# A two-layer graph network with residual and layernorm: the order of each engine's instructions from a planner at build time, and layer 1's products in float32r halves, two node tiles to a pass

## The chip, the cores and the metric

The kernel runs on one core of one Trainium2 chip. The core has a matrix engine (TensorE, PE in the profile, with PEld for its weight loads), a vector engine (VectorE, DVE), a scalar engine (ScalarE, ACT), a general one (GpSimd, POOL) and SyncE (SP), which here only issues transfers. Each executes its own list of instructions in the order in which the program issued them; semaphores connect the lists. The metric is the device time of one execution in microseconds, the median of several.

## The reference

There are 6250 nodes with 256 features, and 100000 edges sorted by destination. Destinations are drawn as 6250 u², u uniform, so low-numbered nodes have many more edges than high-numbered ones. In float32:

```
def agg(h, eps):                 # GIN aggregation
    return (1 + eps) * h + segment_sum(h[src], dst)
h   = relu(agg(x, eps1) @ W1a + b1a)     # 256 -> 512
h1  = relu(h @ W1b + b1b)                # 512 -> 512
h   = relu(agg(h1, eps2) @ W2a + b2a)    # 512 -> 512
y   = h @ W2b + b2b                      # 512 -> 256
out = layernorm(x + y)                   # eps 1e-5, no scale or shift
```

## The kernel before, in words

Nodes come in 49 tiles of 128 (the last has 106). Edges come in chunks of 128. Both layers have the same structure, and each aggregation is done in two ways.

*Edges to higher nodes* (502 chunks) are gathered: POOL issues one indirect DMA per chunk (`gather`, L262 to L278, the DMA at L270), which fetches 128 rows of x or of h1. Chunks come in pieces of four, six pieces are in flight, and piece i + 6 may not be issued before the sums of piece i. PE adds the 128 rows into at most 32 slots by a product with a 0/1 matrix `sel` (L1087). Groups of up to 20 chunks make one such set of sums; ACT copies it (`split`, L1111, or L535 and L536 in layer 2), PE spreads it over 128 nodes by a second 0/1 matrix `to` (L1136), and DVE adds it to the accumulators `acc` of the tiles it reaches (L1125). Groups run from the highest nodes to the lowest.

*Edges to the seven lowest tiles* ("heavy", 280 chunks) are counted. DVE makes two 0/1 masks per chunk, `ca` (L919) and `cb` (L922), PE multiplies them (L961), and DVE adds the counts to `at` at an offset read at run time (L935). The table `at` holds four node tiles in a ring (`RING`); ACT turns a tile's counts into float32 (`cf`, L946), stores them as uint16 for layer 2 (L951), and DVE zeroes the place for the tile four further down (L948). PE then multiplies the counts of a tile by all 49 tiles of x, in 13 ranges of four node tiles (L869). Layer 1 does this in float32, one heavy tile after the other, and reads x anew for each. Layer 2 loads the stored counts and takes h1 as two float32r halves: `upper`, rounded by ACT (L535), and the rest, by DVE (L536).

*Dense work* is done on blocks of one or two tiles (`block`, L717): transposes (L746), a copy `zt` (L755), the first product (L778), relu with bias (`ht`, L787), the second product (L799), and the finish: layer 1 adds the bias on DVE (L1162), applies relu on ACT (L1166) and writes h1; layer 2 adds bias and residual and normalises (L1191 to L1208). Accumulators are loaded by `seed` (L616) into eight block buffers and scaled by ACT (L634).

Layer 2's gathers read arbitrary rows of h1, so the first of them waits for the last write of layer 1.

The order of each engine's list is set while the kernel is built, with the framework's own scheduling off. One loop goes through the pieces (L1071 to L1150). Four times per piece it calls `tick`, which issues what `later` and `take_later` have put off by a fixed number of chunks (`LAG`, ten or seven), and `pump`, which lets two queues, the dense blocks and the heavy tiles' work, issue a step each time their credit allows. `spread` (L124) sets the credit rates, so that dense and heavy work together take an even share.

## Time and profile before

| | us |
|---|---|
| median of three runs | 1387.91 (1386.85 to 1388.59) |
| the profiled execution's time | 1388.87 |
| its span, first to last instruction | 1387.0 |
| layer 1's first and last gather issued | 8.78 and 672.88 |
| layer 2's first and last gather issued | 705.38 and 1348.36 |

In the profile's rows, the number after the start is a duration; brackets hold the idle time before the instruction and what ended it. A row of stretches gives the busy time of each engine with its count of instructions, then the granted PE clock (1.00 is full), the busy share of the DMA engines and GB/s. A row of waits gives the total, the count and the longest. Records of consecutive matmuls overlap, so their mean is more than the time each adds; runs of them in the chain of waits give that time. A float32 matmul has two records.

### The profile page before, as it was taken

The page shows a single profiled execution, that of the slowest core. Times are in us where ns is not written, and L with a number is a line of the kernel's source. Part 1 is how long each engine was busy: PE and PEld are TensorE (multiplying, and loading weights), DVE is VectorE, ACT ScalarE, POOL GpSimd, SP SyncE. Part 2 cuts the span into 40 slices and gives each one's busy share as a digit, 9 for nine tenths or more (in the row PEclk, how much of TensorE's full clock was granted, in tenths as well). Part 3 has the DMA queues.
Part 4 walks back from the last instruction along what each step waited for, and adds up shares of the span by engine and source line. Part 5 has one row for each costly group of instructions (what it writes and reads, how often), then busy time and mean ns, then how long its engine had stood idle before and what let it go on. Part 6 is the DMA issues. An engine that isn't in the chain of part 4 may idle for free.

```text
span 1387.0 us, 19481 instructions
## 1 busy us (share of the span) xinstructions
PE 1264.6 (91%) x6366; PEld 799.7 (58%) x6366; DVE 851.8 (61%) x2208; ACT 457.5 (33%) x871; POOL 975.1 (70%) x1018
## 2 busy tenths in 40 slices
PE   2579999999998999999853999999999999999897
PEld 1136566465655656555531576676666666666666
DVE  7985675768666686711122768868876565665334
ACT  0234253343523324242232333433443333322121
POOL 6777776677677677777347777777777776777760
PEclk9989999999999999999986999999999999999999
DMA  4668687586775847785379797998898898977771
GB/s 110 194 213 267 199 252 245 159 251 202 243 236 168 275 154 223 213 277 179 119 274 302 248 307 248 303 300 286 251 321 291 281 306 275 305 238 233 233 236 41
DMA packets 181091, 328.05 MB, mean 237 GB/s; under 512 B 26425, under 2 KB 112631, under 8 KB 180981
## 3 DMA queue, kind: packets, MB, share of 16 engines
q0 software_dynamic: 64256, 197.46, 45.9%
q1 hardware_dynamic: 94312, 103.36, 22.9%
q10 hardware_dynamic: 22412, 25.89, 5.4%
q8 instruction: 54, 0.88, 0.3%
q14 instruction: 57, 0.46, 0.1%
HBM read 296.18 MB, written 30.44 MB: 235 GB/s over the span
## 4 chain that ended last, share of the span: by engine, by line
PE 79%; DVE 9%; DMA 6%; POOL 2%; issue 2%; ACT 1%; DVEq 0%; ACTq 0%; SPq 0%; POOLq 0%
PE bank L869 21%; PE bank L799 18%; PE bank L778 17%; PE bank L1087 12%; PE bank L1136 5%; PE bank L961 3%; PE bank L746 2%; DMA early<-h,srcs 2%; DMA late<-h,srcs 2%; DVE at L935 2%; POOL early L270 1%; DMA xr<-in_x_dram 1%; DVE acc L1125 1%; DVE cb L922 1%; POOL late L270 1%
## 5 line engine op out<-in xcount | busy, mean ns | idle before, releaser
L270 POOL DMA_INDIRECT early<-in_x_dram,srcs x502 | 487.8, 972 | 182.8 <-issue 124.7
L270 POOL DMA_INDIRECT early<-h,srcs x250 | 240.8, 963 | 112.4 <-issue 95.1
L869 PE MATMUL bank<-xr,cf 128*128 128x256 f32 (+2 forms) x1029 | 304.7, 392 | 13.6 <-DMA xr<-in_x_dram 4.3
L270 POOL DMA_INDIRECT late<-h,srcs x252 | 243.9, 968 | 78.3 <-issue 63.1
L1125 DVE SCALAR_TENSOR_TENSOR acc<-bank,mask,acc 128x256 f32<-128x256 f32 (+1 forms) x420 | 231.4, 607 | 80.6 <-PE bank L1136 80.4
L869 PEld LDWEIGHTS bank<-xr,cf 128*128 128x128 f32 (+1 forms) x1029 | 196.0, 193 | 57.8 <-issue 12.4
L778 PE MATMUL bank<-zt,w2a_s 128*128 128x256 f32 (+2 forms) x832 | 178.8, 373 | 2.1 <-ACT zt L755 2.1
L799 PE MATMUL bank<-w1b_s,ht 128*128 128x512 f32 (+1 forms) x392 | 176.7, 598 | 0.0
L778 PEld LDWEIGHTS bank<-zt,w2a_s 128*128 128x128 f32 x832 | 151.9, 194 | 36.0 <-DVE acc L1125 3.9
L1087 PE MATMUL bank<-early,sel 128*32 128x256 f32 (+1 forms) x1504 | 152.2, 479 | 19.2 <-DVE sel L654 10.1
L869 PE MATMUL bank<-upper,cf 128*128 128x512 f32 (+1 forms) x343 | 143.2, 417 | 14.6 <-DMA ci<-counts 11.6
L1136 PE MATMUL bank<-split,to 128*128 128x256 f32 (+3 forms) x360 | 120.3, 438 | 24.7 <-ACT split L535 21.1
L935 DVE TENSOR_TENSOR at<-bank,at 128x490 f32 x173 | 115.3, 667 | 32.8 <-PE bank L961 14.0
L799 PEld LDWEIGHTS bank<-w1b_s,ht 128*128 128x128 f32 (+1 forms) x392 | 73.4, 191 | 86.3 <-issue 79.7
L1136 PEld LDWEIGHTS bank<-split,to 128*128 128x128 f32 (+1 forms) x360 | 65.7, 199 | 73.6 <-ACT split L535 28.6
L876 DVE TENSOR_TENSOR acc<-bank,acc 128x512 f32<-128x512 f32 (+1 forms) x98 | 64.8, 665 | 65.8 <-PE bank L869 65.5
L922 DVE TENSOR_SCALAR cb<-numbers,spot 128x490 f16<-128x490 f16 x280 | 103.1, 368 | 0.0
L654 DVE TENSOR_TENSOR sel<-iota,slot 128x256 f32<-128x256 f32 (+2 forms) x118 | 50.7, 430 | 84.1 <-PE bank L1087 83.3
L536 DVE TENSOR_TENSOR split<-bank,split 128x512 fp32r<-128x512 f32 (+1 forms) x90 | 61.1, 681 | 64.0 <-ACT split L535 63.9
L869 PEld LDWEIGHTS bank<-upper,cf 128*128 128x128 f32 (+1 forms) x343 | 65.1, 190 | 58.7 <-ACT cf L886 17.5
L961 PE MATMUL bank<-cb,ca 128*128 128x490 f16 x280 | 87.7, 381 | 10.0 <-DVE at L935 6.5
L778 PE MATMUL bank<-zt,w1a_s 128*128 128x256 f32 (+2 forms) x416 | 94.2, 373 | 1.4 <-DVE at L935 1.0
(128 smaller groups left out, 1286.5 us busy)
## 6 DMA issues: line engine op xcount, KB each, us to landing
xr<-in_x_dram SPq DMA_DIRECT2D x84, 512.0 KB
h<-h1r ACTq DMA_DIRECT2D x48, 256.0 KB
xr<-h SPq DMA_DIRECT2D x12, 1024.0 KB
acc<-h SPq DMA_DIRECT2D x22, 512.0 KB
counts<-ci ACTq DMA_DIRECT2D x84, 128.0 KB
ci<-counts SPq DMA_DIRECT2D x84, 128.0 KB
early<-in_x_dram,srcs POOLq DMA_INDIRECT x502
acc<-in_x_dram SPq DMA_DIRECT2D x22, 256.0 KB
```

The source lines that it names most:

```text
L270: nc.gpsimd.indirect_dma_start(out=rows_[:, j, :], out_offset=None, in_=table, in_offset=bass.IndirectOffsetOnAxis(ap=srcs[:, c : c + 1], ...
L536: nc.vector.tensor_tensor(lower, of, upper, op=ALU.subtract)
L778: nc.tensor.matmul(ph[0][:, (f - o) * TILES * P : (f - o) * TILES * P + nb], wa[:, k, f * P : (f + 1) * P], zt[:, k, :nb], start=(k == 0), ...
L799: nc.tensor.matmul(po[0][:m], ht[:, f, i * P : i * P + m], wb[:, f, :], start=(f == 0), stop=(f == KH - 1),)
L869: nc.tensor.matmul(pm[0], cf[:m, j, :], of[:m, j, :], start=(opens and j == 0 and of is not (None if once else xr)), stop=(closes and j == ...
L876: nc.vector.tensor_tensor(acc[t], ap, acc[t], op=ALU.add)
L922: made = nc.vector.tensor_scalar(b, numbers, spot[:, c : c + 1], None, op0=ALU.is_equal)
L935: nc.vector.tensor_tensor(to, ap.rearrange("p (k w) -> p k w", w=W), to, op=ALU.add)
L961: mm = nc.tensor.matmul(pc[0], a, b, start=(i == 0), stop=(i == n - 1))
L1087: mm = nc.tensor.matmul(pm[b * SLOTS : (b + 1) * SLOTS], sel[:, c - c0, :], rows_[:, j, :], start=(c == parts[b][0]), stop=(c == parts[b][ ...
L1125: nc.vector.scalar_tensor_tensor(acc[t], ap[:, i * width : (i + 1) * width], mask[:, t - lo[g], g : g + 1], acc[t], op0=ALU.mult, op1=ALU.add,
L1136: nc.tensor.matmul(pu[0][:, i * width : (i + 1) * width], to[:used], split[:used, l, :], start=(once or l == 0), stop=(once or l == 1),)
```

## The change

**The order.** `Queue`, `later`, `tick`, `pump`, `place` and `spread`'s rates no longer set it. Each piece of work becomes a Python generator that asks for an engine (with an estimated cost and a priority), for a buffer, for an event, or for a rest (an estimated transfer time). A small event simulation, `Plan`, runs while the kernel is built, and grants each engine to the waiting request of the lowest priority number; an instruction is issued at the moment of the grant. On PE the order of priority is: sums of gathered rows (0); merges, counting and layer 1's products (1); dense blocks (2); layer 2's products (3). On DVE and ACT merges come first, and masks and counts last. Nothing of the simulation remains at run time: each engine executes a fixed list and waits on semaphores as before.

```
+LINK = {"PE": 0.4, "DVE": 0.2, "ACT": 0.3}
+GATHER = 1.255
+LANDINGS = (3.0, 6.0)
+LOAD = 6.0
+SUMS = 0.0025
+MERGE = 0.25
+ENDING = 3
+def dve(n):
+    return 0.15 + 0.00105 * n
+def act(n):
+    return 0.18 + 0.00083 * n
...
+    def grant(self, e):
+        if self.free[e] <= self.now and self.asks[e]:
+            _, _, process, cost = heapq.heappop(self.asks[e])
+            self.free[e] = self.ending = self.now + cost
+            ask = self.advance(process)
+            if ask:
+                self.at(self.ending + LINK[e], self.take, process, ask)
+            self.at(self.free[e], self.grant, e)
...
+                    yield ("until", arrived[upto])
+                    yield ("on", "PE", SUMS * width, 0)
...
+                        yield ("on", "ACT", act(n * P) + 0.1, 3)
```

**Layer 1's products.** They use float32r. In the first of four passes (tiles 6 and 5; 4 and 3; 2 and 1; 0) each range of x is loaded, ACT rounds it to one half, DVE forms the other, and both are stored to a new DRAM tile `halves`; the later passes load both halves and ACT copies them once more as float32r. One matmul covers both halves, 512 columns wide, and DVE adds both halves of the result.

```
-                        for of in (xr,) if once else (upper, xr):
-                            nc.tensor.matmul(
-                                pm[0], cf[:m, j, :], of[:m, j, :],
...
+                                yield ("on", "PE", PASS * len(ks) * 2 * width, 1)
...
+                                    nc.tensor.matmul(
+                                        bank[tokens[i].number][:, : 2 * width], cf[:m, j, :],
+                                        xh[:m, j, :, :].rearrange("p a d -> p (a d)"),
+                                        start=(k == 0), stop=(k == NT - 1),
+                                    )
...
+                    for i in range(2):
+                        yield ("on", "DVE", dve(width), 2)
+                        nc.vector.tensor_tensor(
+                            acc[t], ap[:, i * width : (i + 1) * width], acc[t], op=ALU.add
+                        )
```

Four checks of the node numbers are added to the preparation, because counting for a later pass may begin before the ring's old places are cleared, as far as the edges allow.

**Layer 1's finish.** The bias comes in as a float32r matmul of 64 rows, which opens the second product; ACT's relu then reads PSUM directly, and the DVE addition is gone.

```
+                            nc.tensor.matmul(po[:m], twice[:, :m], bias, start=True, stop=False)
...
-            nc.vector.tensor_tensor(y[:m], po[:m], b1b_s[:m], op=ALU.add)
```

**Counting.** The `ca` masks are made for four chunks by one tensor_tensor. Cleared places of `at` are zeroed by ACT, not DVE:

```
+                    yield ("on", "ACT", act(here.shape[1] * P), 4)
+                    nc.scalar.activation(here, here, AF.Copy, scale=0.0)
```

**Layer 2.** Its products go through the ranges from the highest nodes down. The heavy tiles' accumulators start as ACT copies of the first product, and the tile's own scaled rows are added by DVE later (`sowing`, 60 us on). Its plan starts 40 us before its gathers. Tiles that the last three groups reach become blocks of one tile in both layers. Buffers that layer 1 needs only for the heavy tiles, and those that layer 2 needs early, lie in the same part of the memory (`loan`).

More of the change, by code (lines that the diff above doesn't have):

```diff
@@ L27 @@
 RANGE = 4
+PAIR = 2
+BATCH = 4
 PACES = (1.15, 1.4)
@@ new lines, in layer, with settle @@
+            block_of = {t: b for b, ts in enumerate(blocks) for t in ts}
+            passes = PASSES if once else ()
+            need = [
+                sum(uses[t] + ((1 if once else len(ranges)) if t < tiles else 0) for t in ts) + 1
+                for ts in blocks
+            ]
+            acc = {}
+            ready = {t: Event(plan) for t in range(NT)}
+            def settle(t):
+                b = block_of[t]
+                need[b] -= 1
+                if not need[b]:
+                    plan.then(plan.start, dense(b))
@@ L608, in layer @@
[L608 to L636 removed]
+            arrived = {}
```

1386 lines of the change are left out of this document (863 added, 523 removed).

## The prediction

> **What bounds the kernel now.** I read the shares of busy time first, then four stretches cut at the first and last row gather of each layer, then the rows of GpSimd (POOL), which issues the gathers, and its waits, last the chain at the two ends.
>
> ```profile
> PE 1264.6 (91%) x6366; PEld 799.7 (58%) x6366; DVE 851.8 (61%) x2208; ACT 457.5 (33%) x871; POOL 975.1 (70%) x1018
> ```
>
> ```profile
> 8.70:674.00 665.30, 609.00 (x2967) 360.62 (x2968) 428.30 (x1265) 226.88 (x414) 487.79 (x502) 0.98 0.69 214
> 674.00:705.30 31.30, 23.04 (x108) 13.55 (x106) 5.03 (x10) 11.04 (x24) 0.00 (x0) 0.89 0.30 105
> 705.30:1349.50 644.20, 603.61 (x3110) 401.94 (x3111) 399.53 (x791) 211.38 (x411) 484.72 (x502) 0.96 0.86 279
> 1349.50:1387.00 37.50, 28.02 (x181) 23.04 (x180) 14.73 (x38) 8.15 (x23) 0.00 (x0) 0.92 0.16 49
> ```
>
> ```profile
> 8.78 1.13 POOL L270 DMA_INDIRECT early<-in_x_dram,srcs  x1 [5.50 <-DVE rawf L343]
> ...
> 672.88 0.95 POOL L270 DMA_INDIRECT early<-in_x_dram,srcs  x1 [0.30 <-issue]
> 705.38 0.94 POOL L270 DMA_INDIRECT early<-h,srcs  x1 [31.55 <-issue]
> 706.62 0.95 POOL L270 DMA_INDIRECT early<-h,srcs  x1 [0.30 <-issue]
> ...
> 1348.36 0.95 POOL L270 DMA_INDIRECT late<-h,srcs  x1 [0.30 <-issue]
> ```
>
> PE is 91% busy and looks like the bound. POOL is at 70%, yet each gather carries 0.30 us of issue that isn't counted: 0.95 + 0.30 = 1.25 us is the undisturbed step. Layer 1's 501 steps take 672.88 - 8.78 = 664.1 us, 1.326 each; layer 2's take 1348.36 - 705.38 = 643.0 us, 1.283 each. So 501 steps at 1.25, 626 us, are a wall in each layer, and the kernel is two such walls, a hand-over of 31.55 us between them and an end of 37.5 us. What is above the wall is partly PE: a gather reuses its buffer only when PE has summed the rows there.
>
> ```profile
> POOL early L270 <- PE bank L1087: 23.1, 20, 5.7
> POOL early L270 <- PE bank L961: 12.4, 16, 6.0
> ```
>
> ```profile
> POOL early L270 <- PE bank L1087: 6.7, 6, 3.8
> ...
> POOL late L270 <- PE bank L1087: 3.0, 5, 1.7
> ```
>
> The first fence is layer 1, the second layer 2. Take the ordinary 0.30 from each count: 35.5 - 36 x 0.30 = 24.7 us lost to PE in layer 1, 9.7 - 11 x 0.30 = 6.4 in layer 2. The rest above the wall (664.1 - 626 - 24.7 = 13 and 643.0 - 626 - 6.4 = 11) is longer gathers, and stays. The change can therefore win about 31 us inside the layers, plus what it wins at the ends.
>
> **The change, part by part.**
>
> ```profile
> L869 PE MATMUL bank<-xr,cf 128*128 128x256 f32 x672 | 164.9, 390 | 13.6 <-DMA xr<-in_x_dram 4.3 <-ACT ht L787 3.7 <-ACT split L1111 2.8
> ```
>
> ```profile
> 389.44 1.92 PE bank L869 x8
> ...
> 1085.35 1.85 PE bank L869 x8
> ```
>
> *Layer 1's products.* A float32 matmul is two records, so 672 records are 336 full products, four to a range and tile: 1.92 us. Layer 2 already has float32r products 512 wide: eight took 1.85 us, 0.23 each. (The mean of 390 ns is no price; pipelined records overlap.) The new form needs 4 x 0.23 = 0.93 us where 1.92 stood, so 343 products save 343 x (0.48 - 0.23) = 85 us. The bias as a matmul adds 49 x 0.23 = 11 us, so PE gives up 74 us in layer 1: 609 - 74 = 535 us of work for 640 us of gathering. Even if the plan wastes a tenth of PE, the gathers bound this layer. Of the 24.7 us I take 20 (bounds 0 and 24.7; a loss is the second rival).
>
> ```profile
> L1162 DVE TENSOR_TENSOR h1t<-bank,b1b_s 128x512 f32<-128x512 f32 (+1 forms) x49 | 33.7, 688 | 97.3 <-PE bank L799 97.1
> L919 DVE TENSOR_SCALAR ca<-numbers,low 128x128 f16<-128x128 f16 x280 | 76.3, 273 | 12.7 <-PE bank L961 12.7
> L922 DVE TENSOR_SCALAR cb<-numbers,spot 128x490 f16<-128x490 f16 x280 | 103.1, 368 | 0.0
> L948 DVE MEMSET at<- 128x256 uint32 (+1 forms) x39 | 10.1, 260 | 16.6 <-ACT cf L946 15.1
> L946 ACT CAST cf<-at 128x512 f32<-128x512 uint16 (+1 forms) x91 | 54.1, 595 | 113.2 <-DVE at L935 80.6 <-PE bank L869 13.6 <-DMA xr<-in_x_dram 4.3
> ```
>
> ```profile
> 746.16 1.15 ACT L634 ACTIVATE acc<-acc,e 128x1024 f32<-128x1024 f32 x1 [27.77 <-DMA acc<-h]
> ```
>
> *DVE and ACT.* DVE loses the bias addition (33.7), the memsets (10.1) and 280 small `ca` masks (76.3) for 70 of four times the width, each between 0.37 (the 490-wide mask) and 0.69 (a 512-wide tensor_tensor): 26 to 48 us; I take 48. It gains 13 subtractions for the halves of x, 1024 wide, two of 0.69 each: 18 us; and 7 second additions. In all about -50 on 428. ACT gains 13 halving casts (1.15 each at 1024 wide, 15 us), 39 rounding copies of reloaded halves at twice that (90 us) and 39 clearings at 0.6 (23 us): 227 becomes about 355 of 640. Neither fills up, so both cost nothing while PE and the gathers run beside them. If that cover were gone, ACT's 2.3 us rounding copies would stand ahead of a merge's copy in ACT's queue, and the gathers' 24 rows of buffer would have to pay.
>
> ```profile
> xr<-in_x_dram SPq DMA_DIRECT2D x84, 512.0 KB
> ```
>
> *DMA.* Seven readings of x (84 x 0.5 MB = 42 MB in whole ranges) become one reading, one storing of halves and three readings at 1 MB a range: 12 x (0.5 + 1 + 3) = 54 MB. 12 MB more on 214 GB/s x 665 us = 142 MB: the DMA share goes from 0.69 to about 0.75, below the 0.86 at which layer 2's gathers keep 1.283. Nothing on the path. The new loads pass SP's queue beside the accumulator loads; a load waiting there for a free buffer holds up the next seed, as 84 such loads do now.
>
> *The start.* Four more checks are eight small DVE instructions before the branch, some 2 us. The first 24 gathers run on beside it, but the first sums then come later by up to that. I take +1 (0 to 2).
>
> ```profile
> 677.44 1.00 PE bank L1087 x16
> 678.44 3.65 PE bank L799 x8
> 682.08 0.02 issue
> 682.11 0.70 DVE h1t L1162
> 682.81 0.02 issue
> 682.83 0.64 ACT h1r L1166
> ...
> 683.86 0.59 ACT split L1111
> 684.45 0.04 issue
> 684.50 2.07 PE bank L1136 x4
> ...
> 700.90 0.70 DVE h1t L1162
> ```
>
> *The hand-over.* The last sums end at 678.44, and their copy by ACT starts at 683.86: in ACT's written order it stands behind the relu of an older tile, which waits for DVE, which waits for PE. The plan gives a merge's copy first place. That takes out up to 5.4 us, and the two bias additions on this chain 1.4 more; the bias matmuls put back 0.5. Take -5 (-9, with a tighter end, to +4, where an older tile's last block comes to stand before the final ones). Layer 2's PE work no longer stands still after it:
>
> ```profile
> 750.88 1.51 PE L1136 MATMUL bank<-split,to 64*128 64x512 f32 x2 [21.11 <-ACT split L535]
> ```
>
> ACT waits 27.77 us there for accumulator rows that SP fetched late, and PE 21.11 us behind ACT. The new kernel issues them ahead, and starts its products with the high ranges, written long before. That frees PE, but POOL lost only 6.4 us in this layer: take -4 (-6.4 to 0). The heavy tiles' own rows are now added by seven DVE instructions some 60 us later instead of scaled by ACT at the start; DVE is busy 399.5 of 644.2 us there, so they hide.
>
> ```profile
> 1356.97 0.99 PE bank L1087 x8
> 1357.96 3.77 PE bank L778 x32
> 1361.73 0.69 PE bank L1136 x2
> ```
>
> ```profile
> 1357.89 3.84 PE L778 MATMUL bank<-zt,w2a_s 128*128 128x128 f32 x32
> ...
> 1366.66 5.47 PE L778 MATMUL bank<-zt,w2a_s 128*128 128x128 f32 x32 [2.08 <-ACT zt L755]
> ```
>
> *The end.* The last gather leaves at 1349.3; its sums run at 1356.97 behind other tiles' blocks, and the merge behind another 3.77 us. Sums and merges come first in the plan, some 6 us sooner, but the heavy tiles' blocks must still find room: -5 (-9 to +6).
>
> Sum: -20 + 1 - 5 - 4 - 5 = -33 us on a span of 1387.0, to 1354. This execution took 1388.87, 1.9 more than its span; the median of the runs is 1387.91. From the median: 1355.
>
> **The rivals.**
>
> *PE stays the bound in layer 1.* The last fence shows the same 32 records take 3.84 us, and 5.47 after an idle 2.08: a gap costs 1.6 us more, at a lower clock. The freed 105 us (640 - 535) may come as gaps of some 2 us; 105 / 3.7 = 28 of them eat it. Then layer 1 keeps its 664 us, and only the ends win: -13, 1375. For it: the plan is exact where the chip is not. Against it: a gap at which PE waits for rows means that POOL is the bound already, and the gathers run 24 rows ahead. The Trainium skill (TensorE: Matmul & The Clock Gate, "What's actually happening") says that the clock halves only after an idle window of about 3.4 us; by that rule such gaps cost nothing more and the sum stands. The row above disagrees, with 2.08 us.
>
> *Slower: the heavy tiles' chain outlasts the gathers.* Counting must finish two tiles before their pass, and tiles share a ring of four, so counting for 2, 1 and then 0 waits until 6, 5 and then 4 are copied out and cleared. A pass takes ACT 13 x (2 x 3 x 0.6 + 2.3) = 77 us; two such waits are 153. DVE has about 378 us of work in this layer and counting stands last in its order, so with no idle time at all it ends near 31 + 378 + 153 = 562, and the last pass near 562 + 13 x 3.5 = 608, 45 before the gathers' new end near 653. DVE now idles 665 - 428 = 237 us. Let 90 of these fall into the chain, and it ends 45 us late; with its block of 12 us the hand-over slips by some 50: 1405. It is slower than before once it slips by 33. Against: counting need not wait for all of a pass, and DVE's other work isn't all ahead of it.
>
> *No change worth measuring.* The plan's costs miss, its first-come order hands back at merges and seeds what it wins: 1388.
>
> **How the numbers follow.** The forecast 0.68 (own range 1338 to 1373: all bounds that gain, -24.7 - 9 - 6.4 - 9 = -49, give 1339); PE still the bound 0.12; no change 0.07; the slow chain 0.13. Below 0.2%, 2.8 us, a measurement of this kernel tells nothing. Of the no-change case 0.06 lies within that and 0.01 beyond it on the fast side. Faster: 0.68 + 0.12 + 0.01 = 0.81; same 0.06; slower 0.13. A range of 1338 to 1388 leaves out the slow chain and little more.
>
> **What would show it.** Layer 1's gathers at about 1.28 us a step with under 8 us of waits for PE sums, PE busy there about 535 us; products in fours of some 0.93 us; 25 to 27 us between the layers' gathers; no 21 us wait of PE at layer 2's start; the last gather to the end in 33 us. It is wrong if the step stays at 1.32 with PE busy throughout, or if heavy products run past layer 1's last gather.

## The result, and the profile after

The changed kernel takes 1378.16 us (median of 20 runs, 1374.47 to 1386.57), the kernel before 1386.84 beside it (20 runs, 1381.88 to 1393.25). The ratio is 0.9942, 95% interval 0.9928 to 0.9957: 8.7 us faster. The forecast was 33 us. The profiled execution of the changed kernel took 1377.27 us, its span is 1375.3.

e5 to e8 and e13 to e16 below ran on two chips on which the kernel before itself takes 1609 and 1622 us; their ratios are given, but times are read from the runs beside which it takes 1385 to 1388.

First the page of the changed kernel, shares of busy time:

```profile
PE 1239.8 (90%) x6120; PEld 740.1 (54%) x6120; DVE 832.7 (61%) x1940; ACT 564.5 (41%) x977; POOL 986.1 (72%) x1018
```

Then the gathers on POOL, first and last of each layer, and four stretches cut at them (span of the stretch, busy time of PE, weight loads, DVE, ACT and POOL, then clock, DMA share and GB/s):

```profile
7.57 1.13 POOL L450 DMA_INDIRECT early<-in_x_dram,srcs  x1 [4.30 <-DVE rawf L523]
...
670.10 0.95 POOL L450 DMA_INDIRECT early<-in_x_dram,srcs  x1 [0.30 <-issue]
693.72 1.11 POOL L450 DMA_INDIRECT early<-h,srcs  x1 [22.67 <-DMA h<-h1r]
...
1333.42 0.95 POOL L450 DMA_INDIRECT late<-h,srcs  x1 [0.31 <-issue]
```

```profile
7.57:670.10 662.53, 583.95 (x2718) 306.21 (x2721) 409.95 (x1000) 324.62 (x520) 495.19 (x502) 0.95 0.73 240
670.10:693.72 23.62, 15.58 (x86) 8.52 (x78) 2.40 (x7) 7.66 (x17) 0.95 (x2) 0.99 0.13 45
693.72:1333.42 639.70, 607.91 (x3122) 398.35 (x3123) 403.81 (x796) 223.42 (x418) 486.40 (x502) 0.98 0.86 278
1333.42:1375.30 41.88, 31.43 (x202) 26.39 (x200) 12.14 (x33) 8.75 (x24) 0.95 (x1) 0.93 0.14 45
```

Set against the rows of before, the 11.7 us of span come out so:

| term | before | after | measured | forecast |
|---|---|---|---|---|
| first gather | 8.78 | 7.57 | -1.2 | +1 |
| layer 1, first to last gather | 664.1 | 662.5 | -1.6 | -20 |
| hand-over, idle time before layer 2's first gather | 31.55 | 22.67 | -8.9 | -5 |
| layer 2, first to last gather | 643.0 | 639.7 | -3.3 | -4 |
| start of the last gather to the end | 38.6 | 41.9 | +3.3 | -5 |

The hand-over came better than forecast, layer 2's gathers nearly as forecast. Layer 1 did not, and the end gave back what layer 2's gathers had won: from layer 2's first gather to the end, 681.6 us before and 681.6 after. A second execution of the same kernel (e9 below) has -2.5, -7.0, -6.9 and +3.1 us for the last four rows, so their signs hold, and a difference of 4 us in one term says little. Layer 1 is the larger miss. In the group of its gathers (busy time and mean; then the idle time before them), the kernel before first:

```profile
L270 POOL DMA_INDIRECT early<-in_x_dram,srcs x502 | 487.8, 972 | 182.8 <-issue 124.7
```

```profile
L450 POOL DMA_INDIRECT early<-in_x_dram,srcs x502 | 496.1, 988 | 171.6 <-issue 130.7
```

Idle time fell by 11.2 us, and the gathers themselves grew longer by 8.3. An undisturbed layer would show 502 x 0.95 = 476.9 busy and 501 x 0.30 = 150.3 idle, with the wait for the first indices (4.3 us here) on top: 19 and 17 us are left above the wall of 626.

PE did get freer, though by much less than forecast. Its groups from the first gather to the hand-over, before and after (groups overlap at their ends):

```profile
L799 PE MATMUL bank<-w1b_s,ht 128*128 128x512 f32 (+1 forms) x392 | 176.7, 598 | 0.0
L869 PE MATMUL bank<-xr,cf 128*128 128x256 f32 x686 | 168.9, 390 | 13.6 <-DMA xr<-in_x_dram 4.3 <-ACT ht L787 3.7 <-ACT split L1111 2.8
```

```profile
L1103 PE MATMUL bank<-w1b_s,ht 128*128 128x512 f32 (+1 forms) x392 | 193.7, 619 | 0.0
L1466 PE MATMUL bank<-xh,cf 128*128 128x512 f32 (+1 forms) x343 | 114.7, 455 | 10.6 <-ACT xh L1403 10.5
L1102 PE MATMUL bank<-first_bias,twice 64*128 64x512 f32 (+1 forms) x49 | 25.2, 514 | 0.6 <-DVE at L1599 0.5
```

The products fell by 54 us and not 85, the bias costs 25 and not 11, and the second dense product, now granted in two parts with the bias ahead of the first, rose by 17, which the forecast did not have. And PE, busy 584.0 of 662.5 us, stands still more than before: the idle time before its instructions adds up to 59 us between 50 us and the hand-over, where it was 32 in the kernel before. Its waits in the changed kernel between 45 and 690 us:

```profile
PE bank L1033 <- DVE acc L997: 10.8, 7, 3.1
PE bank L1466 <- ACT xh L1403: 10.5, 6, 2.5
PE bank L987 <- ACT split L973: 9.4, 1, 9.4
PE bank L987 <- ACT split L968: 7.5, 8, 1.9
PE bank L1576 <- ACT split L968: 6.5, 1, 6.5
```

Most name ACT and DVE, hardly any a gathered row: a freed PE waits for the engines that feed it, and gathers still wait for PE.

### The profile page after: what moved, and what is told of

It reads as the page before. It is cut to its first block, busy times and chain, and to the rows that moved or that the text cites. A ratio compares the mean times of both kernels' runs of the same rounds, so it can differ in the third digit from the quotient of the medians.

```text
span 1375.3 us, 18780 instructions
## 1 busy us (share of the span) xinstructions
PE 1239.8 (90%) x6120; PEld 740.1 (54%) x6120; DVE 832.7 (61%) x1940; ACT 564.5 (41%) x977; POOL 986.1 (72%) x1018
## 3 DMA queue, kind: packets, MB, share of 16 engines
q1 hardware_dynamic: 81554, 116.23, 25.2%
## 4 chain that ended last, share of the span: by engine, by line
PE 57%; DMA 17%; POOL 8%; issue 6%; ACT 4%; DVE 4%; ACTq 0%; DVEq 0%; SPq 0%; POOLq 0%
PE bank L1103 15%; PE bank L1072 12%; PE bank L942 9%; PE bank L1313 7%; POOL early L450 5%; PE bank L987 5%; PE bank L1466 4%; DMA early<-h,srcs 4%; PE bank L1576 3%; POOL late L450 3%; DMA late<-h,srcs 3%; DMA acc<-in_x_dram 3%; PE bank L1033 2%; DMA xh<-halves 2%; PE bank L1102 1%
## 5 line engine op out<-in xcount | busy, mean ns | idle before, releaser
L450 POOL DMA_INDIRECT early<-in_x_dram,srcs x502 | 496.1, 988 | 171.6 <-issue 130.7
L997 DVE SCALAR_TENSOR_TENSOR acc<-bank,mask,acc 128x256 f32<-128x256 f32 (+1 forms) x420 | 247.0, 607 | 78.7 <-PE bank L987 77.5
L1103 PE MATMUL bank<-w1b_s,ht 128*128 128x512 f32 (+1 forms) x392 | 193.7, 619 | 0.0
L1072 PEld LDWEIGHTS bank<-zt,w2a_s 128*128 128x128 f32 x864 | 151.8, 192 | 37.1 <-issue 8.4
L1313 PE MATMUL bank<-upper,cf 128*128 128x512 f32 (+1 forms) x343 | 148.6, 433 | 6.0 <-ACT upper L1205 5.1
L1313 PE MATMUL bank<-xr,cf 128*128 128x512 f32 (+1 forms) x343 | 137.6, 401 | 0.0
L1466 PE MATMUL bank<-xh,cf 128*128 128x512 f32 (+1 forms) x343 | 114.7, 455 | 10.6 <-ACT xh L1403 10.5
L1237 ACT CAST cf<-ci 128x512 fp32r<-128x512 uint16 (+1 forms) x91 | 53.8, 595 | 145.6 <-PE bank L1313 108.4
L1103 PE MATMUL bank<-w2b_s,ht 128*128 128x256 f32 (+1 forms) x392 | 102.9, 388 | 0.0
L1538 DVE TENSOR_SCALAR cb<-numbers,spot 128x490 f16<-128x490 f16 x280 | 92.5, 361 | 0.0
L1082 ACT ACTIVATE ht<-bank,b2a_s 128x256 f32<-128x256 f32 (+2 forms) x108 | 44.3, 452 | 116.9 <-PE bank L1072 116.8
L1072 PEld LDWEIGHTS bank<-zt,w1a_s 128*128 128x128 f32 x432 | 79.0, 199 | 22.8 <-ACT zt L1045 7.0
```

Of the source, the lines that this page charges most:

```text
L450: nc.gpsimd.indirect_dma_start(out=rows_[:, j, :], out_offset=None, in_=table, in_offset=bass.IndirectOffsetOnAxis(ap=srcs[:, c : c + 1], ...
L997: nc.vector.scalar_tensor_tensor(acc[t], pu[:, i * width : (i + 1) * width], mask[:, t - lo[g], g : g + 1], acc[t], op0=ALU.mult, op1=ALU.add,
L1072: nc.tensor.matmul(ph[:, (f - o) * TILES * P : (f - o) * TILES * P + nb], wa[:, k, f * P : (f + 1) * P], zt[:, k, :nb], start=(k == 0), st ...
L1103: nc.tensor.matmul(po[:m], ht[:, f, i * P : i * P + m], wb[:, f, :], start=(not once and f == 0), stop=(f == KH - 1),)
L1237: nc.scalar.copy(cf_token.tile[:, :n, :].rearrange("p k j -> p (k j)"), token.tile[:, : n * P],)
L1313: nc.tensor.matmul(bank[token.number][:, :width], cf[:m, j, :], of[:m, j, :], start=(j == 0 and of is upper), stop=(j == len(ks) - 1 and o ...
```

## The experiments

### All but the halves

e1 keeps the planner, two tiles to a pass and every other part of the change, the bias on PE among them, with the products in float32. No run has the order alone.

```
-                xh_room = Tiles(loan, [P, RANGE, 2, width], F32R, "xh", 3)
+                xh_room = Tiles(loan, [P, RANGE, width], F32, "xh", 4)
-                        if ts is PASSES[0]: ... halves ... rounding
+                        in_rows(ks, xh, table)        # x itself, for each pass
```

> The changed kernel with its planner, but layer 1's products in float32 as before: two tiles per pass are kept, x is read anew for each pass, there are no halves, no rounding copies and no DVE subtraction for them. In the changed kernel's trace the 502 gathers of layer 1 take 662.5 us: 626 for 501 steps of 1.25, 21.9 of gathers longer than 0.95 us, 14.5 of idle time. Theory A, the halves are needed to free PE: PE goes back by some 50 us in layer 1 to 650 of 686, PE is the bound there again, the gathers' idle time rises to 25 or more, layer 1's gathers take 672 us or more, the whole 1385 to 1395. Theory B, the gain comes from the order alone and the halves give back on GpSimd what they win on PE: the longer gathers fall to 13 us as before the change, idle time stays near 15, layer 1's gathers take 650 to 658, the whole 1367 to 1376. Hand-over of 23 us and layer 2 of 640 us in both.

1379.8 us, ratio 0.9949 (0.9928 to 0.997): the whole gain of the change, without the halves. The time lies between the two expectations. The group of the gathers, and the stretches to the hand-over:

```profile
L450 POOL DMA_INDIRECT early<-in_x_dram,srcs x502 | 493.4, 983 | 160.9 <-issue 132.5
```

```profile
7.49:656.71 649.22, 606.68 (x2985) 355.89 (x2984) 394.40 (x980) 243.16 (x454) 492.50 (x501) 0.99 0.64 192
656.71:698.81 42.10, 37.08 (x156) 19.58 (x155) 2.27 (x6) 15.20 (x34) 0.95 (x1) 0.97 0.22 78
```

Layer 1's gathers take 13.3 us less than in the changed kernel (Theory B had that, at 650 to 658 us in all), and PE's work is back near 650 us (Theory A had that). That 37 us of it are left after the last gather neither had: both took the hand-over at 23 us. PE is busy for 606.7 + 37.1 = 643.8 us to the hand-over where the changed kernel has 584.0 + 15.6 = 599.5. So the halves do free 44 us of PE, and the layer ends only 5 us sooner (698.8 against 693.7).

### The halves alone

e2 keeps the loops of before and makes only the products float32r, one tile to a pass.

```
-                            cf = dense.tile([P, RANGE, P], F32 if once else F32R, ...)
+                            cf = dense.tile([P, RANGE, P], F32R, ...)
-                        for of in (xr,) if once else (upper, xr):
+                        if once:   # one matmul 512 wide over both halves of a row
+                            nc.tensor.matmul(pm[0], cf[:m, j, :], xh[:m, j] as 512 columns, ...)
```

> The kernel before with its loops and queues, in which only layer 1's products go in float32r halves, one tile per pass: x is read once, its halves are stored and read back at 1 MB a range for each of the other six tiles, and rounded by ACT. For room the counting masks have 6 buffers where they had 12, and layer 1's factors 3 where they had 4. Theory A, PE bounds layer 1: PE falls by 85 us there, the gathers' idle time falls from 24.4 us towards 10, the whole takes 1370 to 1380. Theory B, the old order cannot use a freed PE, because ACT stands in its written order at the rounding of a range that has not landed and the merges' copies stand behind it: PE falls by 85 us but the gathers' idle time rises above 24 us, and the whole takes 1390 to 1420.

1560.19 us, ratio 1.1253 (1.1222 to 1.1285). Theory B for the wait, and far beyond its range; PE's busy time in layer 1 fell only to 601 us, from 609, at a granted clock of 0.86. Waits of ACT and of POOL in layer 1:

```profile
ACT xh L874 <- DMA xh<-halves: 95.7, 40, 6.9
```

```profile
POOL early L270 <- PE bank L1146: 170.2, 42, 14.2
```

ACT stands 95.7 us at roundings of ranges that have not landed, and the gathers stand 170 us behind PE's sums. The buffers for two ranges and one tile to a pass are part of this, so it says that the loops cannot take the halves in this form, not that no loop could.

### The bias first, and whole grants

```
 # e3: the block that makes first_bias stands ahead of the index preparation
 # e4
-                        if not f % 2:
-                            yield ("on", "PE", PASS * wide * (8 + (once and not f)), 2)
+                        if not f:
+                            yield ("on", "PE", PASS * wide * (16 + once), 2)
```

> The changed kernel with one thing moved: the bias of layer 1 (its transfers, its cast by ACT with the load of ACT's table, its subtraction by DVE) is prepared before the index preparation, not just ahead of the branch into the ordered part. Theory A, that preparation holds up the branch: PE's first sums come at 33 instead of 38 us, the gathers' one wait of 4.35 us at 39 us falls under 1, layer 1's gathers take 658 us, the whole is 4 us less than with the change, 1374. Theory B, the four added checks on DVE hold it up: first sums stay at 37 to 38 us and the time at 1378.

1384.83 us, ratio 0.9983 (0.9964 to 1.0002): 6 us worse than the changed kernel. Neither theory. The PE rows of e3 at the start (idle time in brackets):

```profile
35.52 0.23 PE L688 MATMUL fp<-bad,ones 128*1 128x19 f32 x2 [15.61 <-DVE bad L684]
37.65 1.92 PE L943 MATMUL bank<-early,sel 128*32 128x256 f32 x12 [1.90 <-SPq L1890]
```

The step from the last check to the first sums now costs 1.9 us of idle time (7.3 in the changed kernel), so the bias did hold up the branch. But the index preparation ends 5 us later, and the first sums come at 37.65 us as they did at 38.02: the cost only moved. That explains a time that did not fall, not the 6 us that it rose; layer 1's gathers took 667.4 us, and the cause of that stays open.

> The changed kernel, in which the planner grants PE to a tile's second dense product whole, sixteen records at a time where it granted eight. Nothing else is changed, but the planner's order moves with it. In the changed kernel's trace these products take 193.7 us of PE in layer 1 and 102.9 in layer 2, where they took 176.7 and 92.6 before the change. Theory A, weight loads at each switch of PE between groups are what ate part of the saving, and layer 2 is full on PE: PE falls by 15 us in layer 1 and 10 in layer 2, the last gather is followed by 36 us instead of 41, the whole is 5 us less, 1373. Theory B, the finer grants keep the sums from standing behind long blocks: PE falls just so, but the gathers' idle time in layer 1 rises by 5 us or more, and the whole is 1378 to 1385.

1397.31 us, ratio 1.0068 (1.0032 to 1.0104): slower than before. Theory B for the wait, more than expected, but not for PE: the product's own group fell from 193.7 to 183.2 us, PE's work to the hand-over did not (604.5 us, 599.5 in the changed kernel). The gathers wait:

```profile
L450 POOL DMA_INDIRECT early<-in_x_dram,srcs x502 | 497.7, 991 | 186.6 <-issue 128.0
```

Idle time rose by 15 us over the changed kernel's. So some 10 of the 17 us by which this product rose are for the two parts. That they keep the sums from standing behind 16 records fits the longer wait, but the whole order changed with the grant.

### Reloads, the subtraction, the estimates

```
 # e5, e10: no transfer for passes 2 to 4; the rounding copy reads w1a instead of xh
-                            in_rows(ks, xh.bitcast(F32)..., halves...)
 # e6: the lower half is a second cast of x
-                            nc.vector.tensor_tensor(xh[:m, js, 1, :], raw..., xh[:m, js, 0, :], op=ALU.subtract)
+                            nc.scalar.copy(xh[:m, js, 1, :], raw.tile[:m, js, :])
 # e7, e11
-GATHER = 1.255   LOAD = 6.0   BEGINS = (0.0, -40.0)
+GATHER = 1.28    LOAD = 9.0   BEGINS = (30.0, -40.0)   # and 20.0 -> 1.0 ahead of x's first load
```

> The changed kernel, in the planner's same order, without the 39 transfers that read the halves of x back for the second to fourth pass of layer 1: ACT's rounding copies stay, but read the first weights, which lie on the chip, so what those passes multiply is not x and the output is not the reference's. In the changed kernel PE stands still for 59.4 us between 50 us and the end of layer 1's work, 10.5 of it for these copies, and the gathers are idle for 15 us and longer than 0.95 us by 20. Theory A, the transfers land later than the plan's 9 us, ACT stands at them in its order, and the slip is passed on to splits, accumulators and sums: PE's stalls fall under 35 us, the gathers' idle time under 8, layer 1's gathers take 652 us, the whole 1364 to 1369. Theory B, the traffic makes the gathers themselves longer: the 20 us fall to 12 and the idle time stays. Theory C, it is the order and ACT's copies, not the transfers: nothing moves by more than 3 us.

> The changed kernel without DVE's 13 subtractions that make the lower halves of x in layer 1 (two operands in SBUF, 1024 wide, 1.14 to 1.23 us each): ACT casts x a second time in their place, so the lower half is a second copy of x and the output is not the reference's. In the changed kernel 21 gathers overlap such a subtraction and are 0.32 us longer on average, 6.8 us in all, and 14 of them last 1.3 to 2.0 us. Theory A, such a subtraction holds up the gather beside it: the long gathers between 140 and 280 us go, the sum of what the gathers are longer falls from 20 to 13 us, the time by some 6, to 1372. Theory B, the gathers are longer through the loads and stores that run at the same time: the sum stays at 20.

> The changed kernel with the planner's estimates set by the trace of the changed kernel: a transfer 9 us (was 6; 12 for the reloaded halves, was 9), a gather 1.28 (was 1.255), and layer 1's first transfers from the moment the engines begin, 30 (was 0). Theory A, the stalls come from estimates that are too short: PE's 59.4 us of stalls in layer 1 fall under 30, its first wait for ACT of 9.4 us falls under 4, the gathers' idle time falls from 15 to under 8, the whole takes 1366 to 1372. Theory B, each order that the planner finds has stalls of its own, whatever its estimates: the stalls stay at 45 us or more and the time falls anywhere between 1370 and 1390.

These came out at ratios of 1.0006 (0.9969 to 1.0042), 1.0046 (1.0015 to 1.0076) and 1.0024 (0.9995 to 1.0052), on the chip where the kernel before took 1609 us. The times say little; one row does. The gathers of e5, e6 and e7, in this order:

```profile
L450 POOL DMA_INDIRECT early<-in_x_dram,srcs x502 | 497.8, 992 | 273.5 <-issue 131.0
```

```profile
L450 POOL DMA_INDIRECT early<-in_x_dram,srcs x502 | 487.8, 972 | 279.9 <-issue 129.8
```

```profile
L450 POOL DMA_INDIRECT early<-in_x_dram,srcs x502 | 496.8, 990 | 272.8 <-issue 132.2
```

Without DVE's subtraction the gathers are as long as before the change, 487.8; without the reloads they stay long, so the reloads are not the cause. But the 9 us between e6 and e7 are no price of the subtraction: e1 has none and its gathers take 493.4, and in e7 the 24 gathers beside a subtraction are longer by 1.6 us in all. Counted gather by gather, the 21 that run beside a subtraction in the changed kernel are longer than 0.95 us by 6.8 us in all (1.6 to 8.1 in the other runs with it). One of them in the changed kernel, with the subtraction beside it:

```profile
222.54 1.98 POOL L450 DMA_INDIRECT early<-in_x_dram,srcs  x1 [0.30 <-issue]
```

```profile
222.48 1.22 DVE L1383 TENSOR_TENSOR xh<-raw,xh 128x1024 fp32r<-128x1024 f32 x1
```

The gather takes its 0.95 us and nearly the whole of the subtraction besides. The Trainium skill (SBUF — State Buffer, "SBUF: two separate sides") says that DVE and GpSimd share a pair of ports as an exclusive lock, and that a DVE instruction with two operands in SBUF holds it throughout against a GpSimd operation that reads SBUF. By that rule this is what should happen, and the rows agree.

A second such instruction is DVE's mask `ca`, which the change made wide: a tensor_tensor with both operands in SBUF. Its group in layer 1, and one with nothing else of DVE beside the gather:

```profile
L1530 DVE TENSOR_TENSOR ca<-numbers,low 128x512 f16<-128x512 f16 x70 | 47.9, 684 | 0.0
```

```profile
249.81 1.38 POOL L450 DMA_INDIRECT early<-in_x_dram,srcs  x1 [0.30 <-issue]
```

```profile
249.68 0.69 DVE L1530 TENSOR_TENSOR ca<-numbers,low 128x512 f16<-128x512 f16 x1
```

In the changed kernel the 89 gathers beside such a mask (and no subtraction) take 1.02 us on average; in e1, 86 take 1.08. The 98 with no DVE instruction beside them take 0.95 and none takes longer, and the same holds for the 39 beside the addition to `at` alone, which has one operand in PSUM. In the changed kernel the gathers beside the wide masks are longer by 5.8 us together, about as much as those beside the narrow ones before (186 gathers, 5.7 us); in e1 it is 11 us, most of the 16.5 by which its gathers are longer than 502 x 0.95. No run has the planner with the narrow masks. The time of e6 did not fall with its gathers (1.0046, where e5 and e7 have 1.0006 and 1.0024), so what the subtractions cost the whole kernel is not shown.

The same questions again, beside the changed kernel itself:

> The changed kernel itself, as the measure for the three runs beside it: in the runs of the four kernels before these the kernel before took 1609 us on that chip instead of 1386, and each engine stood still for long at issue or at a release that the profile could not name, so that ratios there say little of this change. If this chip is as the first one, it takes 0.994 of the kernel before; if it is as the last one, its ratio there, 0.99 to 1.01, says what the others have to be measured against.

> The kernel without the 39 transfers that read the halves back (ACT's copies read the first weights, the output is not the reference's), against the changed kernel on the same chip. On the last chip its gathers were longer than 0.95 us by 20.8 us in layer 1, so traffic does not make them longer. Theory A, late transfers cause PE's stalls in layer 1: against the changed kernel beside it PE's stalls between 50 us and the hand-over fall from 59 under 35 us, the gathers' idle time from 15 under 8, the time by 9 to 14 us. Theory C, order and copies cause them: not over 3 us less.

> The planner with estimates from the trace (transfers 9 us, 12 for the halves, a gather 1.28, layer 1's first transfers from 30 us), against the changed kernel on the same chip. Theory A, too short estimates make the stalls: PE's stalls in layer 1 fall from 59 under 30 us, the time by 6 to 12 us. Theory B, each order has stalls of its own: 45 us or more of stalls, the time within 8 us of the changed kernel on either side.

The changed kernel: 1377.5 us, 0.9934 (0.9899 to 0.9968). Without reloads: 1367.12, 0.9842 (0.9802 to 0.9882). With the estimates: 1369.35, 0.9852 (0.9809 to 0.9895). Gathers of the three, in this order:

```profile
L450 POOL DMA_INDIRECT early<-in_x_dram,srcs x502 | 498.5, 993 | 168.3 <-issue 132.5
```

```profile
L450 POOL DMA_INDIRECT early<-in_x_dram,srcs x502 | 498.2, 992 | 161.1 <-issue 135.3
```

```profile
L450 POOL DMA_INDIRECT early<-in_x_dram,srcs x502 | 498.5, 993 | 161.4 <-issue 131.3
```

Each takes 7 us of idle time from the gathers and leaves their length alone. That reloads come later than the plan's 9 us shows in the two that stand on the chain of waits of the changed kernel:

```profile
579.52 11.63 DMA xh<-halves
...
595.27 9.33 DMA xh<-halves
```

Theory A holds for the medians and for the gathers' idle time, in both. The profiled executions show less of it: 1374.3 us for the changed kernel, 1371.1 and 1373.2 for the two, since the hand-over gives back 2 us without reloads and 8 with the estimates. So the rows bear out 3 and 1 us of the medians' 10 and 8, and where the rest comes from stays open. Theory A does not hold for PE's own stalls, which should have halved: 65 us in this run of the changed kernel (59 in the first), 57 without reloads, 55 with the estimates. The cause that they name changes somewhat: without reloads 9.9 us are for rows from the gathers (6.3 in e9). With the estimates the wait of 9.4 us at the start is gone.

### The bias on DVE, in the order of float32

```
 # e8, e12: on e1
-                            nc.tensor.matmul(po[:m], twice[:, :m], bias, start=True, stop=False)
+                            nc.vector.tensor_tensor(y[:m], po[:m], bias[:m], op=ALU.add)
```

> The kernel of the planner alone (float32 products, x read for each pass), with the bias of layer 1 added by DVE as before the change in place of the matmul on PE. In the run of the planner alone PE is busy for 643.8 us to the hand-over with 19 us of stalls, the gathers end at 656.7 us, and 41.2 us pass to the next gather, 37 of them PE working off what is left. Theory A, in that order PE's sum of work sets the end of layer 1: 25 us less of it for the bias (49 of 0.51 us) shorten the hand-over to 25 us or less, the gathers stay at 649 us, the whole takes 1356 to 1364, faster than the changed kernel. Theory B, DVE's 49 additions of 0.7 us come between its other work, and PE and the gathers wait for it: PE's stalls rise by 15 us or more and the time is 1372 or more.

> The planner alone (float32 products) with the bias added by DVE, against the changed kernel on the same chip. Theory A, in that order PE's sum of work sets the end of layer 1: PE's work there falls from 644 to 619 us, the hand-over from 41 to 25 us, the time is 14 to 20 us under the changed kernel's. Theory B, DVE's additions hold up PE and the gathers: PE's stalls rise from 19 to 34 us or more and the time is within 5 us of the changed kernel's.

e8, on the chip with 1609 us, 1.0055 (1.0023 to 1.0087). The changed kernel did not run there; against e5 to e7 (1.0006 to 1.0046) it is no faster, so there Theory A finds no support. e12: 1365.0 us, 0.9834 (0.9794 to 0.9874), 12.5 us under the changed kernel beside it. Theory A, a little short of its range:

```profile
9.54:653.31 643.77, 592.84 (x2979) 355.72 (x2979) 420.23 (x1022) 247.61 (x459) 489.14 (x502) 0.99 0.65 196
653.31:682.86 29.55, 25.12 (x112) 13.88 (x110) 5.84 (x12) 10.96 (x25) 0.95 (x2) 0.98 0.19 66
```

```profile
53.59 2.37 PE L978 MATMUL bank<-split,to 64*128 64x256 f32 x4 [15.76 <-ACT split L964]
```

PE's work to the hand-over falls from 643.8 to 618.0 us, and the layer ends 16 us sooner. One wait at the start stands out: ACT is at accumulator rows that have not landed, and PE behind it for 15.8 us.

### Both, and a neighbouring order

e13 and e17 put the estimates of e11 on e12; e14 and e16 add the whole grants of e4 to e12 and to e13; e15 and e18 are the changed kernel with `LOAD = 6.2`.

> Float32 products and the bias on DVE (ratio 0.983 before), with the planner's estimates set by the trace (transfers 9 us, a gather 1.28, first transfers from 30 us). In that kernel PE stands still for 38.6 us in layer 1, 15.8 of it once at the start for ACT's copy of the first sums, and 28.6 us pass at the hand-over. Theory A, what is left of stalls comes from estimates: the wait of 15.8 us falls under 6, the hand-over to 24, the whole to 1352 to 1360. Theory B, the order has found its level, layer 1 is bound by PE's sum of work and GpSimd's 1.25 us a step: within 4 us of 1365.

> Float32 products and the bias on DVE, with PE granted whole to the second dense product (16 records). In the changed kernel this grant cost 19 us. Theory A, a long grant keeps the sums waiting whatever else is done: here too the gathers' idle time in layer 1 rises from 2 to 15 us or more, the whole to 1378 or more. Theory B, that loss came with the rounding copies and the late reloads, which are not in this kernel: PE's work falls by 15 us in layer 1, the hand-over to 23 us, the whole to 1355 to 1361.

> The changed kernel with the plan's estimate of a transfer at 6.2 us where it is 6.0, and nothing else: a change of no meaning that gives the planner another order (2,938 lines of difference in PE's list). It measures how far one order and its neighbour lie apart. Theory A, the order is robust: within 3 us of the changed kernel's 1378. Theory B, first come, first served makes it a matter of luck: 5 to 20 us to either side, and a difference of some us between two planned kernels is then no measure of what was changed in them.

> Float32 products, the bias on DVE, estimates from the trace, and the second dense product granted whole: the two edits of the runs beside it together. If their gains add, 1348 to 1356; if long grants cost the sums, 1375 or more; if the order is a matter of luck, anywhere between.

The four ran where the kernel before took 1622 us: 0.9963 (0.9927 to 0.9999), 1.0071 (1.0027 to 1.0115), 1.0042 (1.0006 to 1.0078), 1.0036 (1.0001 to 1.0071). Against each other, e16 is 12.4 us slower than e13 (1627.87 against 1615.45): whole grants cost there too, without halves or reloads. e14 has no kernel without the grants beside it and settles nothing alone. And e13, without halves, is 13 us under e15, which has them (1615.45 against 1628.73).

> Float32 products, the bias on DVE and estimates from the trace once more, in the hope of a chip on which the kernel before takes 1387 us and not 1622. Without the new estimates its ratio was 0.983 there. Theory A, estimates explain the stalls that are left: the wait of 15.8 us at the start falls under 6, the whole to 1352 to 1360. Theory B, the order has found its level: within 4 us of 1365.

> The changed kernel with 6.2 for 6.0 as the plan's estimate of a transfer, once more for the same reason. Theory A, the order is robust: within 3 us of 1378. Theory B, a neighbouring order lies 5 to 20 us to either side.

e18: 1379.16 us, 0.9952 (0.9933 to 0.997). Theory A: an order with some 2,900 other lines in PE's list takes the same time, so a difference of 9 us between two planned kernels need not be luck of the order. It is one neighbour, and e3, with a change outside the plan, came out 6 us longer.

e17: 1361.9 us, 0.9823 (0.98 to 0.9846), the lowest of all, faster than both kernels; e12's interval overlaps with its own.

```profile
L450 POOL DMA_INDIRECT early<-in_x_dram,srcs x502 | 493.4, 983 | 158.7 <-issue 132.2
```

```profile
37.49 2.37 PE L978 MATMUL bank<-split,to 64*128 64x256 f32 x4
```

```profile
1326.44 0.95 POOL L450 DMA_INDIRECT late<-h,srcs  x1 [0.31 <-issue]
```

The wait of 15.8 us is gone, and the gathers' idle time is down to 158.7 us, of which 150.3 are their ordinary 0.30 and the rest is nearly all for the first indices. The time is only 3 us under e12's and within Theory B's 4: layer 1 is bound by GpSimd (645.1 us, of which 18.6 are longer gathers above the wall), and longer gathers there ate what the start gave. The end is 8 us shorter than in e12 (1360.2 - 1326.4 = 33.8 against 41.7), but layer 2's gathers take 5 us more (640.5 against 635.6): from layer 2's first gather on it is 3 us, which layer 1 and the hand-over, 1 and 2 us longer, take back. The two profiled executions take the same time, 1361.9 and 1362.1 us.

## Why the prediction was wrong

*What bounds the kernel: right.* Layer 1 and layer 2 are walls of 626 us with a hand-over and an end, and no kernel here came under them: the shortest are 643.8 us in layer 1 (e12) and 633.9 in layer 2 (e1).

*Layer 1's products, -20: the step that failed.* It read 24.7 us of waits for PE as won if PE is freed, and took the other 13 us above the wall, longer gathers, as fixed. Both halves were wrong: the waits fell by 9.9 us only, the gathers grew longer by 8.3, and -1.6 is left. Of the waits, 24.7 us before, 14.8 are left (27.1 less 41 x 0.30; 11.6 in e9), here as POOL's waits in the changed kernel:

```profile
POOL early L450 <- PE bank L942: 21.3, 22, 4.3
POOL early L450 <- PE bank L1576: 3.4, 11, 0.3
POOL early L450 <- PE bank L1466: 2.4, 8, 0.3
```

They are left because PE has to be fed: PE's work was taken to shrink from 609 to 535 us and 105 us to be spare, where nothing else could be late. It came to 584, and 78 of 662 us were idle (32 of them before 50 us), at ACT's roundings, copies and DVE's additions. That the halves and what they need on the other engines keep the gathers from gaining is shown by e1: without them layer 1's gathers take 13.3 us less, though PE has 44 us more to do. Late reloads account for 7 us of the gathers' idle time (e10), estimates below what the transfers take for 7 (e11); the two overlap and are not to be added. The longer gathers grew by 8.3 us; 6.8 of these fall to the 13 subtractions, which the working counted as 18 us on DVE that cost nothing: they do not run free beside the gathers.

*PE's terms.* The price of a product was nearly right in the chain of waits (runs of four take 0.91 to 1.13 us, forecast 0.93), but as groups the products saved 54 us and not 85, and of PE's work the halves took 44 (e1); the bias cost 25 and not 11 (taking it away in e12 gave back 25.8), 0.5 us for each and not the 0.23 of one in a row of eight, for a reason that no run shows; the second product's +17 was missing, some 10 of it from its two parts (e4). To the hand-over PE fell by 32 us (632.0 to 599.5): the rest of the change added 12, with the bias on PE in it (e1, 643.8), the halves took 44.

*DVE and ACT.* "Neither fills up, so both cost nothing" is the sentence that misled. ACT is busy 325 of 662 us, as forecast about half, and still holds up PE (the waits above): in a written order an engine at half load does so whenever it stands at something late. The working named this price ("the gathers' 24 rows of buffer would have to pay") and then gave it no number.

*Start, +1.* It came out at -1.2 for the first gather. The first sums came at 38.0 us, 32.9 before: not by the four checks, since the last one stands at 30.5 us (30.8 before), but by the bias of layer 1 ahead of the branch, which the working did not cost at all: in e12, without it, the first sums follow the last check by 2.1 us, here by 7.6. The gathers' wait of 4.35 us at 39 us, inside layer 1's term, goes with it.

*Hand-over, -5: right in sign, larger.* It came to -8.9, at the edge of its bounds. It mostly goes with the work that PE does after the last gather: 15.6 us here, 25.1 in e12 and 37.1 in e1, for 22.7, 28.6 and 41.2 us between the gathers; in e17 21.1 us of work go with 30.6. The working had looked at the order of the last copies only. Layer 2's standstill of 21 us is gone, and -4 came as -3.3.

*The end, -5: wrong sign, within its bounds (-9 to +6).* The chain of waits of the changed kernel:

```profile
1340.85 1.00 PE bank L942 x8
1341.84 1.98 PE bank L1072 x16
1343.83 0.87 PE bank L1103 x4
1345.15 1.78 PE bank L1072 x16
1347.80 1.85 PE bank L1313 x8
1349.65 2.60 PE bank L1103 x12
1356.20 7.41 PE bank L1072 x64
```

Sums came first as forecast, 7.4 us after the last gather. Then other tiles' blocks and even heavy products (L1313) run for another 12 us before the last tiles' blocks begin: the backlog stands behind the sums now instead of ahead of them. The working saw this ("must still find room") and had it in the bound, not in the term. PE is busy for 607.9 of layer 2's 639.7 us and 31.4 at the end, 639.3 in all, where it was 631.6 before, with the second product the largest rise (92.6 to 102.9 us in this layer). That this sum of work decides is not borne out: from layer 2's first gather to the end e1 takes 675.8 us with 638.0 of PE's work, e17 674.3 with 638.7, where the changed kernel takes 681.6, and 677.8 in e9. What sets the end stays open.

*The rivals.* The first, 1375 us, was the nearest: layer 1 kept its 664 us, and of the ends the hand-over won. Its mechanism was half there. PE stood in gaps, and gaps of some 2 us do halve the clock for a while, as it says (the last section has the count); but a granted clock that fell from 0.98 to 0.95 over this layer is not what kept it long, since e9, the same kernel, has more gaps (65 us of them against 59) at 0.98 and the same 662 us:

```profile
7.46:669.04 661.58, 577.77 (x2730) 301.49 (x2729) 409.06 (x1000) 324.56 (x520) 497.52 (x501) 0.98 0.74 240
```

And PE was not the bound, since it was idle for 78 us and since 44 us of its work more or less (e1) moved the end of the layer by 5. That the heavy chain outlasts the gathers did not happen: its products end at 628 us, before the last gather. The sign that the forecast had named, a step that stays at 1.32 us, did come (662.5 / 501), without the busy PE that it expected beside it.

## What to carry to other kernels

Before you count an engine's freed time as won, ask which engine is the wall and what the freed work is replaced by on the others: here 44 us of PE were bought with a DVE instruction that holds up GpSimd's gathers and with transfers that come late, and plain float32 products under the same planner, with the bias back on DVE, are faster (0.983 of the kernel before) than the halves (0.994), though on one of the slower chips they were not (e8). In a fixed order, utilisation does not tell whether an engine costs nothing; the time for which others wait for it does. Setting a planner's estimates of transfers from a trace was worth 8 us of the median with the halves and 3, within the noise, without. Test the order and the arithmetic of such a change apart from one another, since each can hide what the other gives back.

## What the runs showed of the hardware

- A DVE instruction with both operands in SBUF can stretch a gather issued beside it: a subtraction of 1.22 us from 0.95 to 1.98 us, a mask of 0.69 us to 1.38. The 21 gathers beside the 13 subtractions were longer by 6.8 us in all in the changed kernel. No gather without a DVE instruction beside it, and none of the 39 beside an addition with one operand in PSUM alone, took longer than 0.95 us there.
- The clock of PE is granted in steps of 3.41 us here, whole or half. In the changed kernel's trace after 40 us, the 16 steps in which it falls to half follow 3.41 us in which PE stood still for 1.66 us or more in all; of the 347 steps that stay whole none follows more than 1.74.
- The 49 matmuls of the bias, each at the head of another product, cost PE 25.2 us as a group and 25.8 us in what e12 gave back, 0.5 each, against 0.23 us in a row of eight. Granting the second dense product whole brought its group from 193.7 to 183.2 us; yet it made the kernel 19 us slower.
- Two chips ran each kernel that also ran on a faster one 16 to 19% slower. The gathers there have the same durations (496.8 us in e7 against 498.5 for the same kernel in e11), but their engine stands still longer between them: idle time before the gathers is 272.8 us instead of 161.4, with the same share at issue (132.2 and 131.3). What causes it stays open.
